# A depthwise convolution split into an input projection and three banded matmuls per output row

## The chip, the core and the metric

The kernel runs on one core of a Trainium2 chip. A core has five engines that matter here, each with its own queue of instructions that it works through strictly in order: PE (TensorE, the matrix engine; its weight loads are listed apart as PEld), DVE (VectorE), ACT (ScalarE), POOL (GpSimd) and SP (SyncE), which issues every DMA of this kernel. Engines wait for each other through semaphores. Data lies in SBUF (128 partitions) and matmuls write to PSUM, which the other engines read.

The metric is the time of one execution on the device in microseconds, as the median of a few executions. Before the change it is 15807.45 us (three executions: 15804.3, 15807.45 and 15817.56).

## The reference, cut to what matters

The input is `x` of shape 2 x 256 x 256 x 128 in fp32. Layer 0 is an attention along each image row; its result is added to `x`. Layer 1, which the change touches, is a selective state-space block:

```python
xz = x @ in_proj_w.T                      # 128 -> 512 channels
xi, z = jnp.split(xz, 2, axis=-1)         # 256 and 256
xi = conv_general_dilated(xi, conv_w, (1, 1), 'SAME', feature_group_count=256) + conv_b
xi = silu(xi)                             # 3x3 depthwise convolution, then silu
...                                       # delta, B, C from xi by small projections
h = dA_t * h + dBx_t                      # 16 states a channel, along all H*W tokens
y = sum over states of h * C + Ds * xi
...                                       # layer norm, times silu(z), projection to 128
```

The input of layer 1 is group-normalised, which the kernel does with one scale and one shift for each of the 128 channels. So for each of 256 inner channels the kernel needs a projection over 128 channels followed by nine taps, three rows by three columns.

## The kernel before, in words

The kernel does layer 0 first, then layer 1 in 128 steps of R = 4 image rows, T = 1024 tokens. Everything is fp32. In the trace one fp32 matmul is two instructions on PE, each with its own weight load.

**Units and slots.** The scan of a step is cut into 32 units of 128 partitions by 1024 tokens: two halves h of 128 channels, in each four groups m of four states, in each four groups q of 32 channels (CQ = 32; 32 channels by SR = 4 states fill the partitions). The last loop of the file (L1130 and following) goes over slots t, one for each unit, and emits the instructions of a slot in a fixed order. Nothing re-orders them later: on PE, DVE, ACT and POOL the program order is the queue order. In a slot come

- the DMAs of six units ahead (`fetch`, on SP);
- `drive`, on POOL, in odd slots: for the pair of units t+3 and t+4 the product `hb` of `du` and `bb` (L1048);
- `products`, on POOL, for five of the 16 pairs of a step, units 6, 14, 22, 26 and 30 with their neighbours (L1084), and a single one for unit 11;
- `decay`, on ACT, for unit t+1: `da` = exp(delta * A) into PSUM (L1038). There are two `da` tiles, so decay of unit t+1 waits until unit t-1 is through with its own;
- `scan` on DVE for unit t (L1060), and, where the unit is not one of POOL's, `product` on DVE (L1075) into `yc`. `yc` tiles hold a pair of units and there are four;
- the pieces of other work that were put into this slot by `at(...)`: first those without `pe=True`, then those with it;
- `start_up` and `add_up` on PE: `add_up` (L1107) sums four units over their states into `y`, and comes in slots 2, 6, 10, 14, ... It frees two of the four `yc` tiles;
- `remember` on ACT, which keeps the last column of the scan (L1065), and at times `y_out`.

**Work put between.** `project(k)` prepares step k: load of the rows, transposes (`turn`), normalisation into `xn` on ACT, then the convolution, the gate `z`, the small projections and three table functions on ACT (`silu_z`, `silu_xs`, `softplus`), each with two table loads. It starts 72 slots before the first scan of its step. `finish_row` does the layer norm and the output of the rows of the step before, from eight slots to eight slots. All pieces of `project` beyond the first step share one PSUM bank ("p"), those of `finish_row` another ("f"): a piece on PE waits until ACT has copied the piece before out of the bank.

In slots counted from 0 to 31 within a step, `project` has its pieces there: `turn` and `normalise` in 24 to 26, the gates in 16 to 18 and 26, `silu_z` in 20, `silu_xs` in 28, the `xd` and `dt` projections in 0 to 3 and 8 to 11, `softplus` in 12. The four convolution blocks of a step (half h by row pair i) begin in slots 27, 3, 11 and 19.

**The convolution before.** The projection and the taps are one set of weights: `w_tap[:, h, tap, :]` is the projection scaled by the tap of each inner channel. A block is nine matmuls (18 instructions) of 128 x 128 weights on 512 columns, shifted windows of `xn`, accumulated in one PSUM tile `u_ps` (L736). They are spread over four slots as 3, 3, 2 and 1 taps; `conv_out` (L747) copies the tile out with the bias five slots after the first. `xn` has two columns of zeros for the border.

## Time and profile before

| what | value |
|---|---|
| executions | 15804.3, 15807.45, 15817.56 us |
| span of the profiled execution, first to last instruction | 15811.9 us, 4.5 us above the median |
| layer 0 and the preparation of the first steps, up to the first scan | 0 to 2631.16 us |
| one step of the scan in the trace, from the scan of unit 11 to that of the next step | 8005.94 to 8108.39 us: 102.45 us |
| convolution matmuls L736, 9216 | 4237.6 us busy, 600 ns each |
| scans L1060, 4096 | 9536.1 us busy, some 2340 ns each |
| decay L1038, 4096 | 4581.5 us busy, 1119 ns each |
| granted TensorE clock | 0.925 on average |

Busy time is the union of the time in which an instruction of the group runs. Matmuls overlap: the end of each is modelled, so the pace of a row of matmuls is read from the starts, and 600 ns is longer than the step from one to the next. In the answers on waits, a line names the waiting instruction, the one that released it, the total in us, the number of times and the longest. In the lines of a timeline the columns are start, duration, engine, source line, operation, what it writes from what, how many; a bracket at the end has the idle time before and what ended it.

### The profile page before, as it was taken

The page shows a single profiled execution, that of the slowest core. Times are in us where ns is not written, and L with a number is a line of the kernel's source. Part 1 is how long each engine was busy: PE and PEld are TensorE (multiplying, and loading weights), DVE is VectorE, ACT ScalarE, POOL GpSimd, SP SyncE. Part 2 cuts the span into 40 slices and gives each one's busy share as a digit, 9 for nine tenths or more (in the row PEclk, how much of TensorE's full clock was granted, in tenths as well). Part 3 has the DMA queues.
Part 4 walks back from the last instruction along what each step waited for, and adds up shares of the span by engine and source line. Part 5 has one row for each costly group of instructions (what it writes and reads, how often), then busy time and mean ns, then how long its engine had stood idle before and what let it go on. Part 6 is the DMA issues. An engine that isn't in the chain of part 4 may idle for free. (4 is left out here: it accounts for less than half of the span.)

```text
span 15811.9 us, 177304 instructions
## 1 busy us (share of the span) xinstructions
PE 13767.7 (87%) x59451; PEld 6979.9 (44%) x59451; DVE 14381.3 (91%) x12134; ACT 10831.9 (69%) x20003; POOL 13322.4 (84%) x3216
## 2 busy tenths in 40 slices
PE   6999998888888888888888888888888888888887
PEld 5877884333333333333333333333333333333333
DVE  6665555999999999999999999999999999999998
ACT  4555555777777777777777677777777777777775
POOL 1111113999999999999999999999999999999998
PEclk8999998999999999999999999999999999999998
DMA  5322223777676776767677667777677777776765
GB/s 194 126 97 82 81 96 121 242 246 240 239 242 241 243 244 241 240 240 245 241 245 244 230 237 244 242 243 244 241 240 243 245 242 243 246 240 241 243 244 194
DMA packets 1426852, 3452.05 MB, mean 218 GB/s; under 512 B 117736, under 2 KB 709136, under 8 KB 1405456
## 3 DMA queue, kind: packets, MB, share of 16 engines
q1 hardware_dynamic: 1425936, 3440.72, 62.7%
q8 instruction: 467, 7.65, 0.2%
q14 instruction: 449, 3.68, 0.1%
HBM read 2752.41 MB, written 687.88 MB: 218 GB/s over the span
## 5 line engine op out<-in xcount | busy, mean ns | idle before, releaser
L1048 POOL TENSOR_TENSOR hb<-du_r,bb 128x2048 f32<-128x2048 f32 x2048 | 9247.5, 4543 | 87.8 <-DMA du_r<-du_d 16.1
L1060 DVE TENSOR_TENSOR_SCAN da<-da,state,hb 128x1024 f32<-128x1024 f32 x2688 | 6301.6, 2344 | 3.5 <-POOL state L1139 3.2
L1038 ACT ACTIVATE da<-delta_r,a_neg 128x1024 f32<-128x1024 f32 x4096 | 4581.5, 1119 | 85.1 <-DMA delta_r<-delta_d 6.0
L736 PE MATMUL u_ps<-xn,w_tap 128*128 128x512 f32 x9216 | 4237.6, 600 | 27.1 <-ACT sz L773 24.1
L1075 DVE TENSOR_TENSOR yc<-da,cc 128x1024 f32<-128x1024 f32 x2688 | 3284.5, 1222 | 253.2 <-PE y L1107 99.1
L1060 DVE TENSOR_TENSOR_SCAN hb<-da,state,hb 128x1024 f32<-128x1024 f32 x1408 | 3234.5, 2335 | 79.6 <-ACT state L1065 65.0
L1084 POOL TENSOR_TENSOR yc<-hb,cc 128x2048 f32<-128x2048 f32 x640 | 2906.8, 4542 | 86.1 <-ACT state L1065 66.4
L736 PEld LDWEIGHTS u_ps<-xn,w_tap 128*128 128x128 f32 x9216 | 1672.3, 190 | 2303.3 <-issue 1862.5
L1107 PE MATMUL y<-yc,sel 128*32 128x512 f32 x16384 | 2408.2, 712 | 20.2 <-POOL yc L1084 19.4
L458 POOL TENSOR_TENSOR x1g<-xc,bo_all 128x512 f32<-128x512 f32 x256 | 316.1, 1275 | 1844.9 <-DVE stats L513 1836.2
L1065 ACT COPY state<-da 128x1 f32<-128x1 f32 x2688 | 426.4, 159 | 1858.9 <-DVE yc L1075 1850.9
L1107 PEld LDWEIGHTS y<-yc,sel 128*32 128x32 f32 x16384 | 492.5, 126 | 1926.2 <-issue 1709.2
L762 PE MATMUL z_ps<-xn,w_z 128*128 128x512 f32 x1024 | 751.6, 825 | 625.5 <-ACT sz L773 316.9
L901 PE MATMUL yt<-centre,ys 128*128 128x256 f32 x4096 | 1030.9, 395 | 265.7 <-ACT ob L971 264.9
L408 ACT ACTIVATE e<-s_ps,nmx 128x256 f32<-128x256 f32 x1024 | 477.1, 476 | 971.8 <-DVE nmx L399 873.6
L804 PE MATMUL dt_ps<-xd,w_dt 8*128 8x512 f32 x1024 | 695.8, 764 | 507.2 <-ACT delta L815 414.1
L1065 ACT COPY state<-hb 128x1 f32<-128x1 f32 x1408 | 268.5, 191 | 1058.0 <-DVE hb L1060 1057.9
L901 PEld LDWEIGHTS yt<-centre,ys 128*128 128x128 f32 x4096 | 742.6, 191 | 445.3 <-ACT ob L971 361.5
L954 PE MATMUL o_ps<-w_out,szr 128*128 128x128 f32 x4080 | 790.0, 275 | 0.0
L954 PE MATMUL o_ps<-w_out,yg 128*128 128x128 f32 x4080 | 789.1, 275 | 0.0
L375 DVE TENSOR_TENSOR v<-v_ps,bv_all 128x512 f32<-128x512 f32 x256 | 176.9, 691 | 581.1 <-PE v_ps L368 581.1
L954 PEld LDWEIGHTS o_ps<-w_out,yg 128*128 128x128 f32 x4080 | 660.4, 192 | 26.9
(162 smaller groups left out, 17185.1 us busy)
## 6 DMA issues: line engine op xcount, KB each, us to landing
bb<-bc_d SPq DMA_DIRECT2D x1024, 512.0 KB, 4.1
cc<-bc_d SPq DMA_DIRECT2D x1024, 512.0 KB, 5.3
delta_r<-delta_d SPq DMA_DIRECT2D x1024, 512.0 KB, 6.3
du_r<-du_d SPq DMA_DIRECT2D x1024, 512.0 KB, 5.2
sz_d<-sz SPq DMA_DIRECT2D x128, 1024.0 KB, 6.5
xs_d<-xs SPq DMA_DIRECT2D x128, 1024.0 KB, 9.5
xr<-xs_d SPq DMA_DIRECT2D x256, 512.0 KB, 6.6
delta_d<-delta SPq DMA_DIRECT2D x128, 1024.0 KB, 8.8
```

The costliest lines, as they stand in the source:

```text
L736: nc.tensor.matmul(o["u"], w_tap[:, h, tap, :], xn[:, i * RB + dy : i * RB + dy + RB, dx : dx + W], start=(tap == 0), stop=(tap == 8),)
L762: nc.tensor.matmul(o["z"], w_z[:, h, :], xn[:, 1 + i * RB : 1 + (i + 1) * RB, 1 : W + 1], start=True, stop=True,)
L804: nc.tensor.matmul(o["dt"], w_dt[:, h, :], o["xd"][0:DR, i * TB : (i + 1) * TB], start=True, stop=True,)
L901: nc.tensor.matmul(o["yt"][:, j, :], ys[k, h][:, t0 + j * P : t0 + (j + 1) * P], centre[:, (1 - h) * P : (1 - h) * P + DI], start=(h == 0) ...
L954: nc.tensor.matmul(o["o"][:, j, :], o[by][:, h, j * P : (j + 1) * P], w_out[:, i, h, :], start=False, stop=(j == WT - 1 and h == NH - 1 an ...
L1038: nc.scalar.activation(da, spreads["delta", k, h, q], AF.Exp, scale=a_neg[:, g, m : m + 1])
L1048: nc.gpsimd.tensor_tensor(hb, spreads["pair", k, h, q], repeats["bb", k, h, m].unsqueeze(1).to_broadcast([P, 2, T]), ALU.mult,)
L1060: nc.vector.tensor_tensor_scan(u["h"], u["da"], u["hb"], st, ALU.mult, ALU.add)
L1065: nc.scalar.copy(st, units[t]["h"][:, T - 1 : T])
L1075: eng.tensor_tensor(u["yc"], u["h"], repeats["cc", k, h, m], ALU.mult)
L1084: nc.gpsimd.tensor_tensor(yc, hb, repeats["cc", k, h, m].unsqueeze(1).to_broadcast([P, 2, T]), ALU.mult)
L1107: nc.tensor.matmul(y[q * CQ : (q + 1) * CQ, cols], sel, units[t + q]["yc"][:, cols], start=False, stop=(m == NSG - 1),)
```

## The change: projection first, then three banded matmuls for each row

The projection and the taps become two sets of matmuls.

- **Weights.** `w_tap` goes. `w_in` is the transposed projection. `w_cv[:, g, r, dx, :]` is a matrix of 128 by 32 for channel group g, output row r of two, and column shift dx: its rows are (input row, channel) for four input rows by 32 channels, and it holds the tap of (dy, dx) where the input row is r + dy and the channels agree. It is built at the start from a zeroed tile `cw`, which six DMAs now fill in place of one, and one multiplication on DVE. 18 scalings on DVE, 18 transposes and 18 copies go, two transposes and copies come.
- **`inner(h, i, j)`**, on PE: for two of the four channel groups, the projection of the four input rows of block (h, i) to 32 channels. Each of eight matmuls has 128 x 32 weights and 256 columns, and writes the 32 partitions of its row: the result has (row, channel) on the partitions.
- **`inner_out(j)`**, on ACT: copies these 128 x 512 values into `xin`, which has the zero border columns that `xn` no longer has.
- **`conv(h, i)`**, on PE: for each of two output rows and three column shifts, four matmuls (one for each channel group, each writing its 32 partitions) of 128 x 32 weights on 256 columns.
- **Slots.** In the first slot of a block: `inner` for j = 0 on PE and, by a new list of pieces that come after those of PE, `inner_out(0)` on ACT. In the second: `inner` for j = 1. In the third: `inner_out(1)`, and then all of `conv`. `conv_out` stays five slots after the first. All of it uses the one bank "p" in turn.
- **Memory.** `xd` moves into the buffer of `raw`, which the load of the next rows uses too.

```diff
+    RB = TB // W
+    w_cv = const.tile([P, NCG, RB, 3, CQ], F32, name="w_cv")
...
+        cw = prep.tile([P, NCG, RB, 3], F32, name="cw")
+        nc.vector.memset(cw, 0.0)
+        taps = conv_w.rearrange("(g c) o i j -> c g (o i) j", c=CQ)
+        for r in range(RB):
+            for dy in range(3):
+                nc.sync.dma_start(
+                    out=cw[(r + dy) * CQ : (r + dy + 1) * CQ, :, r, :], in_=taps[:, :, dy, :]
+                )
...
         for h in range(NH):
-            for tap in range(9):
-                wt = prep2.tile([P, P], F32, name="wt")
-                nc.vector.tensor_scalar(wt, inp[:, h, :], cw[:, h, tap : tap + 1], None, ALU.mult)
-                transposed(w_tap[:, h, tap, :], wt, P)
+            transposed(w_in[:, h, :], inp[:, h, :], P)
...
-        def conv(h, i, taps):
-            if taps[0] == 0:
-                o["u"] = bank([P, RB, W], "u_ps")
-            for tap in taps:
-                dy, dx = divmod(tap, 3)
-                nc.tensor.matmul(
-                    o["u"],
-                    w_tap[:, h, tap, :],
-                    xn[:, i * RB + dy : i * RB + dy + RB, dx : dx + W],
-                    start=(tap == 0),
-                    stop=(tap == 8),
-                )
+        def inner(h, i, j):
+
+            o["xi"] = bank([P, 2, W], "xi_ps")
+            for q in range(2):
+                c = (2 * j + q) * CQ
+                for r in range(SR):
+                    nc.tensor.matmul(
+                        o["xi"][r * CQ : (r + 1) * CQ, q, :],
+                        w_in[:, h, c : c + CQ],
+                        xn[:, i * RB + r, :],
+                        start=True,
+                        stop=True,
+                    )
+
+        def inner_out(j):
+            nc.scalar.copy(xin[:, 2 * j : 2 * j + 2, 1 : 1 + W], o["xi"])
+
+        def conv(h, i):
+            o["u"] = bank([P, RB, W], "u_ps")
+            for r in range(RB):
+                for dx in range(3):
+                    for q in range(NQ):
+                        nc.tensor.matmul(
+                            o["u"][q * CQ : (q + 1) * CQ, r, :],
+                            w_cv[:, h * NQ + q, r, dx, :],
+                            xin[:, q, dx : dx + W],
+                            start=(dx == 0),
+                            stop=(dx == 2),
+                        )
...
-                o["xd"] = s1.tile([64, T], F32, name="xd")
+                xd = s1.tile([P, R, WT, C], F32, name="raw")
+                o["xd"] = xd.rearrange("p r t c -> p (r t c)")[0:64, :]
...
-            for dt, taps in ((0, (0, 1, 2)), (1, (3, 4, 5)), (2, (6, 7)), (3, (8,))):
-                at(t + dt, conv, h, i, taps, pe=True)
+            at(t, inner, h, i, 0, pe=True)
+            at(t, inner_out, 0, after=True)
+            at(t + 1, inner, h, i, 1, pe=True)
+            at(t + 2, inner_out, 1)
+            at(t + 2, conv, h, i, pe=True)
             at(t + 5, conv_out, h, i)
...
-            others, on_pe = slots.pop(t, ((), ()))
-            for piece, args in others:
-                piece(*args)
-            for piece, args in on_pe:
+            others, on_pe, after = slots.pop(t, ((), (), ()))
+            for piece, args in (*others, *on_pe, *after):
                 piece(*args)
```

More of the change, by code (lines that the diff above doesn't have):

```diff
@@ L132, in attn_then_ssm_kernel @@
     lnb_c = columns("lnb_c", ln_b)
-    w_tap = const.tile([P, NH, 9, P], F32, name="w_tap")
+    w_in = const.tile([P, NH, P], F32, name="w_in")
     w_z = const.tile([P, NH, P], F32, name="w_z")
@@ L159, in attn_then_ssm_kernel @@
         nc.sync.dma_start(out=inp, in_=in_proj_w.rearrange("(k p) c -> p k c", p=P))
-        cw = prep.tile([P, NH, 9], F32, name="cw")
-        nc.sync.dma_start(out=cw, in_=conv_w.rearrange("(h p) o i j -> p h (o i j)", p=P))
+        cw = prep.tile([P, NCG, RB, 3], F32, name="cw")
[6 more added lines that the diff above has]
+                )
+        same = prep.tile([P, CQ], F32, name="same")
+        nc.vector.tensor_reduce(
+            same, ident.rearrange("p (r c) -> p c r", c=CQ), AX.X, ALU.add
+        )
+        nc.vector.tensor_tensor(
+            w_cv.rearrange("p g r d c -> p (g r d) c"),
+            same.unsqueeze(1).to_broadcast([P, NCG * RB * 3, CQ]),
+            cw.rearrange("p g r d -> p (g r d)").unsqueeze(2).to_broadcast([P, NCG * RB * 3, CQ]),
+            ALU.mult,
+        )
         outp = prep.tile([P, DI], F32, name="outp")
@@ L631, in attn_then_ssm_kernel @@
     WP = W + 2
-    RB = TB // W
     WT = W // P
@@ L655, in attn_then_ssm_kernel, with at @@
     between = {}
-    def at(t, piece, *args, pe=False):
-        slots.setdefault(t, ([], []))[pe].append((piece, args))
-    xn = s1.tile([P, R + 2, WP], F32, name="xn")
+    def at(t, piece, *args, pe=False, after=False):
+        slots.setdefault(t, ([], [], []))[2 if after else pe].append((piece, args))
+    xn = s1.tile([P, R + 2, W], F32, name="xn")
     nc.gpsimd.memset(xn, 0.0)
+    xin = s1.tile([P, NQ, WP], F32, name="xin")
+    nc.gpsimd.memset(xin, 0.0)
     given = {}
@@ L700, in begin @@
                 if k > 0:
-                    nc.gpsimd.memset(xn[:, 0, 1 : W + 1], 0.0)
+                    nc.gpsimd.memset(xn[:, 0, :], 0.0)
                 first = s1.tile([P, WT, C], F32, name="ob")
@@ L709, in begin @@
             else:
-                nc.scalar.copy(xn[:, 0:2, 1 : W + 1], xn[:, R : R + 2, 1 : W + 1])
+                nc.scalar.copy(xn[:, 0:2, :], xn[:, R : R + 2, :])
             if n < R:
-                nc.gpsimd.memset(xn[:, 2 + n, 1 : W + 1], 0.0)
+                nc.gpsimd.memset(xn[:, 2 + n, :], 0.0)
         def turn(src, r, m):
@@ L723, in normalise @@
             nc.scalar.activation(
-                xn[:, to : to + m, 1 : W + 1],
+                xn[:, to : to + m, :],
                 o["t"][:, 0:m, :],
@@ L729, in normalise @@
             )
-        def conv(h, i, taps):
-            if taps[0] == 0:
-                o["u"] = bank([P, RB, W], "u_ps")
-            for tap in taps:
-                dy, dx = divmod(tap, 3)
-                nc.tensor.matmul(
-                    o["u"],
-                    w_tap[:, h, tap, :],
-                    xn[:, i * RB + dy : i * RB + dy + RB, dx : dx + W],
-                    start=(tap == 0),
-                    stop=(tap == 8),
-                )
+        def inner(h, i, j):
[9 more added lines that the diff above has]
+                        stop=True,
+                    )
+        def inner_out(j):
[11 more added lines that the diff above has]
+                            stop=(dx == 2),
+                        )
         def conv_out(h, i):
@@ L764, in gate @@
                 w_z[:, h, :],
-                xn[:, 1 + i * RB : 1 + (i + 1) * RB, 1 : W + 1],
+                xn[:, 1 + i * RB : 1 + (i + 1) * RB, :],
                 start=True,
```

## The prediction

> **What bounds the kernel now.** I read the page's engine line first, then busy times by stretch, then the waits of DVE and POOL between 4000 and 14000 us (97.6 steps), and last the timelines of one step.

> ```profile
> PE 13767.7 (87%) x59451; PEld 6979.9 (44%) x59451; DVE 14381.3 (91%) x12134; ACT 10831.9 (69%) x20003; POOL 13322.4 (84%) x3216
> 2500.00:15600.00 13100.00, 11298.06 (x45481) 5033.07 (x45482) 12641.47 (x7277) 9334.18 (x16157) 12836.28 (x2913) 0.92 0.70 240
> ...
> DVE yc L1075 <- PE y L1107: 79.3, 99, 1.4
> DVE hb L1060 <- ACT state L1065: 49.8, 96, 0.5
> ...
> POOL yc L1084 <- ACT state L1065: 54.6, 99, 1.8
> ```

> In the scan (second line: PE, PEld, DVE, ACT, POOL, clock, DMA) POOL is busy 98% and DVE 96.5%; PE 86%, ACT 71%. DVE waits 0.8 us a step for PE and 0.5 for ACT, POOL 0.56. So the step of 102.45 us is DVE's row of scans with POOL beside it. PE bounds nothing by its amount: what it does matters only where DVE, or ACT in front of DVE, waits for it.

> Here are slots 10 to 16 of one step; a convolution block begins in slot 11:

> ```profile
> 8004.86 2.07 PE L804 MATMUL dt_ps<-xd,w_dt 8*128 8x512 f32 x2 [2.10 <-ACT delta L815]
> 8006.85 3.33 PE L1107 MATMUL y<-yc,sel 128*32 128x512 f32 x16
> 8010.11 2.84 PE L736 MATMUL u_ps<-xn,w_tap 128*128 128x512 f32 x6
> ...
> 8018.48 1.92 PE L1107 MATMUL y<-yc,sel 128*32 128x512 f32 x16
> ...
> 8008.02 0.68 ACT L815 ACTIVATE delta<-dt_ps,dtb_c 128x512 f32<-128x512 f32 x1
> 8008.59 0.19 ACT L1065 COPY state<-hb 128x1 f32<-128x1 f32 x1
> 8008.67 1.14 ACT L1038 ACTIVATE da<-delta_r,a_neg 128x1024 f32<-128x1024 f32 x1
> 8009.82 1.28 ACT L823 ACT_TABLE_LOAD   x1
> ...
> 8014.53 1.12 ACT L1038 ACTIVATE da<-delta_r,a_neg 128x1024 f32<-128x1024 f32 x1
> ...
> 8011.77 2.35 DVE L1060 TENSOR_TENSOR_SCAN da<-da,state,hb 128x1024 f32<-128x1024 f32 x1
> ...
> 8015.75 4.59 DVE L1060 TENSOR_TENSOR_SCAN hb<-da,state,hb 128x1024 f32<-128x1024 f32 x2
> ```

> See that PE comes to slot 11 only at 8010.11, behind `add_up` of slot 10, while ACT has done slot 11's pieces at 8008.59; and that the `decay` ending at 8015.65 feeds the scan that starts at 8015.75: ACT has no slack there.

> **PE's work.** A block was 18 instructions at some 0.43 us, 8.0 us; four a step, 32 us. It becomes 32 + 48 instructions of 128x32 weights on 256 columns. The nearest row in shape is `y` (128x32, 512 columns):

> ```profile
> 8018.48 0.16 PEld L1107 LDWEIGHTS y<-yc,sel 128*32 128x32 f32 x8 [0.76 <-DVE hb L1060]
> 8018.93 0.13 PEld L1107 LDWEIGHTS y<-yc,sel 128*32 128x32 f32 x4 [0.30 <-issue]
> 8019.36 0.13 PEld L1107 LDWEIGHTS y<-yc,sel 128*32 128x32 f32 x4 [0.30 <-issue]
> ```

> Loads come four together every 0.43 us: four column groups stream side by side, one instruction per 107 ns. With 256 columns I take half, 53 ns. Upper end: 111 ns, the pace of L954 (eight pairs from 8020.87 to 8022.43), since no row shows a load and its matmul going out faster. So `inner` for one j (16) costs 0.85 us (to 1.78), its last result 0.165 us later (592 ns of a `y` matmul less its 427); `conv` (48) costs 2.56 us (to 5.3). A block falls from 8.0 to 4.3 us, some 15 us of PE a step. Alone this is worth nothing: it isn't the bound.
> [...]

> **The added wait.** `inner_out(0)` stands on ACT in the slot in which PE does `inner`. PE reaches that behind `add_up` of the slot before; behind `inner_out(0)` on ACT wait the state copy, the next `decay`, and then often a table function of 4.5 us with the `decay` after it, for which DVE waits. The copy itself costs 0.49 us (the step from the `sz` copy at 8058.94 to the next row at 8059.43).

> - Slot 11: `inner` from 8010.11, result 8011.13; ACT goes on at 8011.65 in place of 8008.59, 3.06 late. `decay`(13) ends 8012.87, so scan 13 goes from 8011.77 to 8012.97. `softplus` follows, `decay`(14) ends 8018.71 instead of 8015.65, scan 14 starts 8018.81: **+3.06 us**.
> - Slot 19: PE's `add_up` of slot 18 lets `inner` start at 8034.31; result 8035.33. ACT's state copy goes from 8034.59 to 8035.85. Scan 21 just holds; `silu_z` follows, and scan 22 (8042.63, already 0.53 late for ACT) becomes **+1.26**.
> - Slot 27: `y` 8058.84 to 8061.71, result of `inner` 8062.73, state copy from 8059.43 to 8063.25. Scan 29 moves from 8062.96 to 8064.56; `silu_xs` follows, scan 30 from 8066.94 to 8070.41: **+3.47**.
> - Slot 3: `y` ends early (8084.94), result 8085.96 against ACT's state copy at 8085.77; no table function follows, `decay`(5) ends by 8088.5 for a scan at 8089.23: **0**.

> Direct sum 7.8 us a step.

> **What is late next.** All of `conv` now waits for `inner_out(1)`, behind that late `decay`: in slot 13 it starts at 8019.25, PE idle since 8012.6. Idle PE restarts slowly here: in the stretch before the first scan, convolution blocks of 18 take 10.12, 9.69 and 9.64 us after gaps, and 7.97 to 8.00 otherwise, so 1.7 to 2.1 us more. I take 4.5 us for `conv` (2.6 to 5.3). Behind it stand `add_up` and the output row.
> - Slot 13: `conv` to 8023.8; the output matmuls end 4.34 later (as 8018.48 to 8022.82 now) at 8028.1, while ACT's `leave`, now 8022.85, would run at 8025.9. ACT wins part of the 2.2 back; at the gate of slot 18 PE is 1.4 behind, which slot 19 hands on in full: **+1.4**.
> - Slot 21: 8043.8 (`decay`(22), with its 1.26) + 0.55 + 4.5 + 1.72 (`start_up`) + 1.9 (`y`) = 8052.5; product 24, which needs that `yc` tile, would run at 8049.57 + 1.26 = 8050.8: **+1.65**. `leave`, the `xn` copy and the normalisations of slots 24 to 26 follow late: scans 26 to 28 lose **0.9**, and product 28's wait for `y` (now 0.76) grows by **0.9**.
> - Slot 29 the same way: no `yc` wait (`y` ends 8077.1, product 0 at 8077.3), but ACT is 1.6 late in slot 0, and slots 3 to 5 lose **1.1**.

> Together 5.9 us a step; nothing if `conv` restarts at full pace.

> **The rest.** POOL and DVE get no work in the scan. ACT's eight copies are in the chains above. SP: the load of `raw` in slot 12 now waits for the `dt` matmul of slot 10, since `xd` lies in the same buffer; behind it are the fetches of six slots ahead, 19 us of cover against 4 to 6 us to land: nothing, and up to 6 us a step without that cover. Before the first scan nine blocks (8 to 10 us) become chains of inner, copy, inner, copy, conv, about 6 to 8: -19 us (-35 to +10). At the start five more DMAs of 0.5 us stand ahead of the loads of x on SP: +3; the scalings and transposes that go lie in DVE's 3.30 us wait for x and give nothing.

> **Sum.** Blocks lie in slots 0 to 4021, 125.7 steps. 125.7 x (7.8 + 5.9) = 1722 us. 15811.9 + 1722 - 19 + 3 = 17518 for the profiled execution, which is 4.5 us (0.03%) above the median of 15807.45: **17515 us**, +10.8%.

> **Rivals.**
> - *Direct stalls alone*: `conv` runs at full pace, its lag is won back in ACT's idle time (ACT waits 2158 us for DVE in the 10000 us). 125.7 x 7.8 - 16 = 964: 16770 us. For it: the clock is granted at 0.92 overall. Against: the gaps of 6 us ahead of `conv`, and slow `y` rows after gaps of 2 us (3.33 for 1.92).
> - *Issue pace*: each load and matmul costs 111 ns. `inner` is 0.9 later in the blocks of slots 11, 19, 27 and 0.4 in slot 3, `conv` 0.8 longer three times: +5.5 us a step, 18200 us. Against: four loads within 0.13 us. That the column groups don't run side by side at all (17 us a block) is excluded by the same rows.
> - *Faster*: PE, 15 us a step lighter, is early everywhere; DVE's 0.8 and ACT's 0.5 go, and POOL, with 54.6 us of waits in 10000, sets the end: 13180 us of scan x 0.55% = 72, about 15735 us. It decides if `inner`'s result is there when ACT comes, that is if PE starts it by 8008.59 - 1.02 = 8007.6 in slot 11. Against: `y` of slot 10 holds PE until 8010.1, behind a `dt` that waits for ACT itself; the change leaves that as it is.
> - *Hidden*: ACT's late `decay` is met by DVE being late too. Against: scan 14 follows its `decay` by 0.1 us.

> **How the numbers follow.** Likeliest case 0.53, its own range 17000 to 17900; direct stalls alone 0.24; issue pace 0.11; smaller stalls, partly absorbed, 0.04; faster 0.06; hidden 0.02. About 0.2% (30 us) is what a measurement here can tell from no change. Slower 0.92, same 0.02, faster 0.06. Range 16550 to 18050: it takes in the direct stalls, and leaves out faster, hidden and the upper half of issue pace.

> **What would show it.** Right: ACT's `xin` copy with idle time released by PE `xi_ps`, 2 to 3 us in slots 11 and 27; DVE's waits for ACT up from 0.5 to 8 us a step or more, at scans 13, 14, 22, 29 and 30; PE's busy share and clock down; POOL under 92% with new waits. `conv` near 4.5 us with slow starts shows the second part, 2.6 the first rival, 5.3 with evenly spaced loads the second. It is wrong if the `xin` copy starts without idle time, or if DVE's waits stay near 1.3 us a step.

## The result, and the profile after

The changed kernel takes **17510.79 us** (median of 17508.42, 17508.69, 17512.89 and 17515.75), against 15806.7 us of the kernel before beside it: a ratio of **1.1077, interval 1.1062 to 1.1092**. The prediction was 17515. One step of the scan, from product 28 to that of the next step, goes from 102.45 to 116.05 us (9000.53 to 9116.58): +13.60, where the prediction's sum was +13.7.

From the page of the changed kernel, the engine line and two of its groups:

```profile
PE 13013.4 (74%) x91179; PEld 6786.8 (39%) x91179; DVE 14474.1 (83%) x12119; ACT 11262.7 (64%) x21011; POOL 13356.8 (76%) x3217
...
L771 PE MATMUL u_ps<-xin,w_cv 128*32 128x256 f32 x24576 | 2383.7, 567 | 2883.3 <-ACT state L1104 2524.1
...
L764 ACT COPY xin<-xi_ps 128x512 f32<-128x512 f32 x1024 | 595.6, 582 | 1227.3 <-PE xi_ps L755 1227.3
```

TensorE is busy for less than before (13013 us, from 13768), DVE and POOL for about the same, and every share has fallen: the engines wait for each other. The granted clock is 0.871 on average, from 0.925. The last column is the idle time ahead of a group. The copies of the inner product wait 1227 us for TensorE, and the convolution stands 2883 us behind waits, nearly all for ScalarE.

The waits of the changed kernel between 4000 and 14000 us (86.2 steps), by DVE, ACT and PE:

```profile
DVE hb L1099 <- ACT da L1077: 519.7, 431, 15.0
DVE yc L1114 <- PE y L1146: 386.2, 345, 2.1
DVE da L1099 <- ACT da L1077: 346.0, 259, 2.0
...
ACT ob L1010 <- PE o_ps L993: 1313.9, 344, 5.6
ACT xin L764 <- PE xi_ps L755: 833.1, 344, 4.1
...
PE u_ps L771 <- ACT state L1104: 1727.2, 258, 7.3
```

Before, DVE waited 0.5 us a step for ACT and 0.8 for PE; now it is (519.7 + 346.0) / 86.2 = 10.0 for ACT's `decay` and 4.5 for `y`. ACT waits 9.7 a step for the inner product, in all four blocks. POOL is busy for 88% of this stretch, from 99%.

Slots 10 to 16 of one step, the place that the prediction showed of before; PE's lines first, then ACT's, then DVE's:

```profile
9052.96 3.64 PE L1146 MATMUL y<-yc,sel 128*32 128x512 f32 x16
9056.38 1.58 PE L755 MATMUL xi_ps<-xn,w_in 128*32 128x256 f32 x16
...
9066.14 5.23 PE L771 MATMUL u_ps<-xin,w_cv 128*32 128x256 f32 x48 [6.40 <-ACT state L1104]
...
9053.54 0.68 ACT L851 ACTIVATE delta<-dt_ps,dtb_c 128x512 f32<-128x512 f32 x1
9058.03 0.58 ACT L764 COPY xin<-xi_ps 128x512 f32<-128x512 f32 x1 [3.81 <-PE xi_ps L755]
9058.51 0.20 ACT L1104 COPY state<-hb 128x1 f32<-128x1 f32 x1
9058.60 1.12 ACT L1077 ACTIVATE da<-delta_r,a_neg 128x1024 f32<-128x1024 f32 x1
9059.74 1.28 ACT L859 ACT_TABLE_LOAD   x1
...
9064.45 1.12 ACT L1077 ACTIVATE da<-delta_r,a_neg 128x1024 f32<-128x1024 f32 x1
...
9056.64 1.22 DVE L1114 TENSOR_TENSOR yc<-da,cc 128x1024 f32<-128x1024 f32 x1 [0.59 <-PE y L1146]
9059.76 2.36 DVE L1099 TENSOR_TENSOR_SCAN da<-da,state,hb 128x1024 f32<-128x1024 f32 x1 [1.90 <-ACT da L1077]
...
9065.67 4.59 DVE L1099 TENSOR_TENSOR_SCAN hb<-da,state,hb 128x1024 f32<-128x1024 f32 x2 [1.85 <-ACT da L1077]
```

Read it from the copy at 9058.03. ACT has been free since 9054.22 and stands for 3.81 us, because `inner` is behind `y`, and both are slow: `y` takes 3.64 us where the row at 9026.82 takes 1.92, `inner` 1.58 where the one at 9028.56 takes 1.05 (the clock granted to TensorE is 0.50 of full speed here, from 9050.63 to 9057.46). Only then come `decay` (to 9059.72; scan 13 starts at 9059.76), the table load and `softplus`, and the next `decay` (to 9065.57; scan 14 starts at 9065.67). And the convolution, which needs the second copy, starts at 9066.14 after 6.40 us without work on PE and takes 5.23 us.

Why so long, the weight loads of another block of the same step show:

```profile
9009.53 0.20 PEld L771 LDWEIGHTS u_ps<-xin,w_cv 128*32 128x32 f32 x8 [6.88 <-ACT state L1104]
9009.96 0.20 PEld L771 LDWEIGHTS u_ps<-xin,w_cv 128*32 128x32 f32 x4 [0.23 <-issue]
9010.39 0.20 PEld L771 LDWEIGHTS u_ps<-xin,w_cv 128*32 128x32 f32 x4 [0.23 <-issue]
...
9012.52 0.20 PEld L771 LDWEIGHTS u_ps<-xin,w_cv 128*32 128x32 f32 x4 [0.23 <-issue]
9012.95 0.62 PEld L771 LDWEIGHTS u_ps<-xin,w_cv 128*32 128x32 f32 x12 [0.23 <-issue]
```

Four loads go out together every 0.43 us for 3.42 us, 107 ns for each load and matmul; from 9012.95 on, 12 take 0.62 us, half of that. The granted clock, asked for in pieces of half a microsecond, says the same: 0.50 from 9006.26 to 9013.08, and 1.00 after. So the pace doubles when the granted clock does; it is not a limit of the issue, since the four of a group come within 0.20 us. In the four blocks of this step the clock rises 3.55, 2.92, 4.97 and 3.90 us after the convolution has begun, and the block at 9066.14, the longest with 5.23 us, is at half pace to its last load. The last section comes back to this.

### The profile page after: what moved, and what is told of

Its sections match the earlier page's. It is cut to its first block, busy times and chain, and to the rows that moved or that the text cites. A ratio compares the mean times of both kernels' runs of the same rounds, so it can differ in the third digit from the quotient of the medians.

```text
span 17506.6 us, 242120 instructions
## 1 busy us (share of the span) xinstructions
PE 13013.4 (74%) x91179; PEld 6786.8 (39%) x91179; DVE 14474.1 (83%) x12119; ACT 11262.7 (64%) x21011; POOL 13356.8 (76%) x3217
## 5 line engine op out<-in xcount | busy, mean ns | idle before, releaser
L771 PE MATMUL u_ps<-xin,w_cv 128*32 128x256 f32 x24576 | 2383.7, 567 | 2883.3 <-ACT state L1104 2524.1
L771 PEld LDWEIGHTS u_ps<-xin,w_cv 128*32 128x32 f32 x24576 | 1039.0, 160 | 4193.8 <-ACT state L1104 2705.7
L1146 PE MATMUL y<-yc,sel 128*32 128x512 f32 x16384 | 2305.9, 684 | 19.5 <-POOL yc L1123 18.7
L1010 ACT COPY ob<-o_ps 128x256 f32<-128x256 f32 x510 | 189.7, 372 | 1909.1 <-PE o_ps L993 1909.1
L764 ACT COPY xin<-xi_ps 128x512 f32<-128x512 f32 x1024 | 595.6, 582 | 1227.3 <-PE xi_ps L755 1227.3
L755 PE MATMUL xi_ps<-xn,w_in 128*32 128x256 f32 x16384 | 1152.0, 402 | 73.1 <-ACT xin L764 5.1
L797 PE MATMUL z_ps<-xn,w_z 128*128 128x512 f32 x1024 | 667.7, 739 | 428.9 <-ACT xn L741 211.0
L840 PE MATMUL dt_ps<-raw,w_dt 8*128 8x512 f32 x1024 | 693.9, 762 | 329.4 <-ACT state L1104 180.0
L755 PEld LDWEIGHTS xi_ps<-xn,w_in 128*32 128x32 f32 x16384 | 507.7, 118 | 817.3 <-issue 325.7
```

Of the source, the lines that this page charges most:

```text
L755: nc.tensor.matmul(o["xi"][r * CQ : (r + 1) * CQ, q, :], w_in[:, h, c : c + CQ], xn[:, i * RB + r, :], start=True, stop=True,)
L771: nc.tensor.matmul(o["u"][q * CQ : (q + 1) * CQ, r, :], w_cv[:, h * NQ + q, r, dx, :], xin[:, q, dx : dx + W], start=(dx == 0), stop=(dx = ...
L797: nc.tensor.matmul(o["z"], w_z[:, h, :], xn[:, 1 + i * RB : 1 + (i + 1) * RB, :], start=True, stop=True,)
L840: nc.tensor.matmul(o["dt"], w_dt[:, h, :], o["xd"][0:DR, i * TB : (i + 1) * TB], start=True, stop=True,)
L1146: nc.tensor.matmul(y[q * CQ : (q + 1) * CQ, cols], sel, units[t + q]["yc"][:, cols], start=False, stop=(m == NSG - 1),)
```

## The experiments

The theory after the result was the prediction's: ACT's wait for the inner product costs about 8 us a step (the direct part), and the convolution, late and at half pace, costs about 5 (the second part). Each is taken away alone, the first is then put into the kernel before, and at the end both are taken away together. All numbers "a step" are the distance to the kernel before in the same comparison, divided by 125.7 steps; the changed kernel stands at 13.6.

**One slot later for the first copy.** Edit against the changed kernel:

```diff
-            at(t, inner_out, 0, after=True)
+            at(t + 1, inner_out, 0)
```

> The changed kernel with one line moved: the first copy of a block, inner_out(0), stands among ACT's pieces of the next slot in place of the end of its own. Nothing else is changed. Theory (the wait of ACT for PE in the slot of the inner product costs 8 to 9 of the 13.6 us that a step grew by, the late conv block most of the rest): ACT no longer waits for xi_ps; what is left is the copy's own 0.5 us ahead of three late decays and part of the late conv block, 3 to 5 us a step, 16200 to 16450 us. Rival (the new matmuls are slow or late in themselves, wherever the copy stands): at least 9 us a step stay, over 16950 us. Rival (the wait alone is the whole loss): under 1 us a step, under 15950 us.

Measured: 16488.23 us, ratio 1.0430 (1.0414 to 1.0445), 38 us above the range. ACT's wait for the inner product falls from 833 to 31 us in the stretch, and 5.4 us a step are left. Moving one copy of each block by one slot wins back 60% of the loss.

**The copy without its wait.**

```diff
         def inner_out(j):
-            nc.scalar.copy(xin[:, 2 * j : 2 * j + 2, 1 : 1 + W], o["xi"])
+            src = o["xi"] if j else xn[:, 0:2, :]
+            nc.scalar.copy(xin[:, 2 * j : 2 * j + 2, 1 : 1 + W], src)
```

> The changed kernel, but the first copy of each block reads xn in place of xi_ps: it stands in the same place and moves as many bytes, and waits for nothing on PE. It leaves out the use of half of the inner product (channel groups 0 and 1 of each half get other values); PE does all of it as before. Theory (the wait): 16400 to 16550 us, the copy's 0.5 us in three blocks and the late conv block stay. Rival (ACT's added work, not its wait): 17300 us or more. ACT's idle time ahead of L764 goes from 833 us in the stretch from 4000 to 14000 us to under 150.

Measured: 16453.54 us (one execution), as expected; 5.1 us a step are left. DVE's waits now:

```profile
DVE yc L1115 <- PE y L1147: 386.7, 271, 3.1
DVE hb L1100 <- ACT da L1078: 189.7, 333, 14.9
DVE da L1100 <- ACT da L1078: 12.5, 36, 1.0
```

The two waits for `decay` go from 866 to 202 us; the wait for `y` stays as it was. The direct part is worth 17510.8 - 16453.5 = 1057 us, 8.4 a step.

**A third of the convolution.**

```diff
-                for dx in range(3):
+                for dx in (1,):
...
-                            start=(dx == 0),
-                            stop=(dx == 2),
+                            start=True,
+                            stop=True,
```

> The changed kernel with a third of the banded matmuls: only the middle column shift, 8 matmuls a block in place of 24, so six of the nine taps are left out. Theory (the conv block of 4.2 to 5.2 us, late behind ACT, costs DVE the waits for yc tiles at units 16 and 24 and some of those at 26 to 28, some 4 us a step; ACT's wait for the inner product stays): a block takes 1.7 us, 16900 to 17150 us. Rival (the length of the block doesn't matter, all of the loss is the direct wait): 17450 us or more.

Measured: 16871.75 us (one execution), 28 below the range. The mirror image of the run before: a block takes 1.07 to 1.94 us, the wait for `y` almost goes (386 to 66 us in the stretch), those for `decay` stay for the most part (866 to 707).

```profile
DVE hb L1099 <- ACT da L1077: 451.9, 410, 12.6
DVE da L1099 <- ACT da L1077: 255.1, 221, 3.1
...
DVE yc L1114 <- PE y L1146: 65.6, 107, 2.2
```

**TensorE kept busy.** The second `inner` is written several times over, the last time with the same numbers, so that PE stands idle for only 1.2 to 1.7 us ahead of the convolution:

```diff
-            for q in range(2):
+            times = (7, 3, 7, 8)[h * NB + i] if j else 1
+            for q in times * (0, 1):
```

> The changed kernel, but the second inner product of a block is done 7, 3, 7 and 8 times over (in the order of the blocks of h and i), with the same result in the same place, so that PE has work until shortly ahead of the conv block. PE does more in all. Theory (a conv block of 48 instructions takes 4.2 to 5.2 us in place of 2.6 because PE stands idle for 3 to 7 us ahead of it): blocks of 2.6 to 3 us, and the time falls by 2 to 4 us a step, to 17000 to 17250 us. Rival (the blocks are slow for another reason, such as the load of 128x32 weights or the reads of xin): blocks as before, 17500 us or more.

Measured: 17002.2 us (16984 to 17041), ratio 1.0752 (1.0734 to 1.077): 21 repeats of the second `inner` in a step, 16 instructions each, make the kernel 509 us faster. One block in PE's timeline:

```profile
9002.79 6.25 PE L756 MATMUL xi_ps<-xn,w_in 128*32 128x256 f32 x112
9010.26 2.80 PE L772 MATMUL u_ps<-xin,w_cv 128*32 128x256 f32 x48 [1.22 <-ACT state L1105]
```

All four blocks of the step take 2.80 us, where they took 4.2 to 5.2 for the same 48 instructions, and the granted clock is 0.948 on average, from 0.871. DVE's wait for `y` falls from 386 to 160. But 9.5 us a step are left, more than the 7.8 of the prediction's direct part alone: DVE still waits 782 us in the stretch for `decay`, 8.8 a step.

**The wait put into the kernel before.** One extra matmul into the bank, a copy of it on ACT in the slot and place where `inner_out(0)` stands, the nine taps as six, two and one from the next slot on; `xd` in the buffer of `raw`, as in the change:

```diff
+        def glance(h, i):
+            o["g"] = bank([P, RB, W], "g_ps")
+            nc.tensor.matmul(
+                o["g"], w_tap[:, h, 0, :], xn[:, i * RB : i * RB + RB, 0:W], start=True, stop=True
+            )
+
+        def seen():
+            nc.scalar.copy(look, o["g"])
...
+            at(t, glance, h, i, pe=True)
+            at(t, seen, after=True)
```

> The kernel before, with the old convolution, and only the wait added: in the first slot of each block PE does one matmul (the first tap, 128x512, 0.86 us and 0.165 us to its result, as the inner product takes) into the bank, and ACT copies its 128x512 values to a tile that nobody reads, in the place of inner_out(0). The nine taps follow in the next slots as six, two and one. xd lies in raw's buffer to make room. Theory (the wait is enough, with the old matmuls too): the 7.8 us a step that were worked out for it before, or up to 10 with what PE does more: 16750 to 17050 us. Rival (the wait is hidden, and the loss came with the new matmuls): under 16000 us.

Measured: 17013.17 us (one execution), 9.6 us a step, in the range. ACT's and DVE's waits:

```profile
ACT look L752 <- PE g_ps L747: 967.7, 357, 4.8
...
DVE hb L1073 <- ACT state L1078: 484.0, 262, 1.9
DVE da L1073 <- ACT da L1051: 370.9, 270, 3.4
DVE yc L1088 <- PE y L1120: 69.9, 157, 2.2
```

The old convolution with a read of PE's result on ACT loses 1206 us, and DVE's wait for `y` stays where it was before (79). So the direct part needs nothing of the new convolution. What was added is a little more than a wait: the copy's own time on ACT and one matmul a block on PE are in the 1206 us.

**The shared buffer alone**, in the kernel before:

```diff
-                o["xd"] = s1.tile([64, T], F32, name="xd")
+                xd = s1.tile([P, R, WT, C], F32, name="raw")
+                o["xd"] = xd.rearrange("p r t c -> p (r t c)")[0:64, :]
```

> The kernel before with one part of the change: xd lies in the buffer of raw. The load of raw then waits on SP for the dt matmul of slot 10. Theory: fetches stand six slots ahead, nothing changes, within 0.2% of before. Rival (SP held up makes delta_r or du_r late): slower by 1 to 6 us a step, 15930 us or more.

Measured: 15806.2 us beside 15806.92, ratio 0.9999 (0.999 to 1.0008). It costs nothing there.

**Two arrangements that should have hidden both parts.** In the first, the pieces move to slots one or two later, and the convolution goes behind `add_up`:

```diff
             at(t, inner, h, i, 0, pe=True)
-            at(t, inner_out, 0, after=True)
-            at(t + 1, inner, h, i, 1, pe=True)
-            at(t + 2, inner_out, 1)
-            at(t + 2, conv, h, i, pe=True)
+            at(t + 2, inner_out, 0)
+            at(t + 2, inner, h, i, 1, pe=True)
+            at(t + 3, inner_out, 1)
+            at(t + 3, conv, h, i, late=True)
```

> The changed kernel with its matmuls and copies as they are, but in other slots: the first copy and the second inner product two slots after the first inner product (so behind the table function and the decay that follows it), the second copy three slots after it, and the conv block there too, but behind add_up, which it now follows on PE. Theory (the loss is only where ACT waits for PE, and what stands behind the late conv block): scans 13, 14, 21, 22, 29 and 30 don't wait more than before, conv starts on a PE that add_up has kept busy and takes about 2.8 us; 0.3 to 2 us a step are left for the output row behind conv, 15850 to 16060 us. Rival (half as much PE work in smaller pieces and eight more copies cost something wherever they stand): over 16400 us. Rival (a lighter PE is worth something once it doesn't stand in the way): under 15770 us, down to the 15735 us that POOL allows.

Measured: 16792.87 us, ratio 1.0623 (1.0605 to 1.064), far off, and slower than moving the one copy. PE's timeline of one block, and one wait of ACT from 4000 to 14000:

```profile
9106.45 1.93 PE L755 MATMUL xi_ps<-xn,w_in 128*32 128x256 f32 x16 [7.77 <-ACT state L1104]
9108.31 2.77 PE L1137 MATMUL y<-xr,d_diag 128*128 128x512 f32 x4
9111.01 1.92 PE L1146 MATMUL y<-yc,sel 128*32 128x512 f32 x16
9112.75 2.77 PE L771 MATMUL u_ps<-xin,w_cv 128*32 128x256 f32 x48
```

```profile
ACT ob L1010 <- PE o_ps L993: 1644.2, 362, 7.5
```

The convolution is at full pace now (2.77 us for its 48), but the slow start has only moved: `inner` waits for the first copy, and after 7.77 us idle it takes 1.93 us (1.05 at 9097.04), and `y` from `xr` behind it 2.77 (1.98 in the changed kernel). The output row stands behind the convolution, and ACT's longest wait for it grows from 5.6 to 7.5 us; scan 26 is 3.05 us late for such a wait in the step from 9000 us.

In the second, the second inner product goes to the other bank ("f"), so that it waits for no copy, both copies come in the fourth slot and the convolution in the fifth:

```diff
-            at(t, inner, h, i, 0, pe=True)
-            at(t, inner_out, 0, after=True)
-            at(t + 1, inner, h, i, 1, pe=True)
-            at(t + 2, inner_out, 1)
-            at(t + 2, conv, h, i, pe=True)
+            at(t + 1, inner, h, i, 0, pe=True)
+            at(t + 2, inner, h, i, 1, pe=True)
+            at(t + 3, inner_out, 0)
+            at(t + 3, inner_out, 1)
+            at(t + 4, conv, h, i, after=True)
```

> The changed kernel with its matmuls and copies as they are, in a third arrangement. The two inner products of a block come in its second and third slot and need no copy between them, since the second takes the bank of the output rows, which is free there; both copies stand in the fourth slot, where ACT has 1 us to spare in the kernel before; conv comes in the fifth, behind add_up and the output row on PE; conv_out stays. Why this is asked: in the arrangement before this one the conv block ran at full pace and scans 13, 14 and 30 no longer waited, yet 7.8 us a step were left; its second inner product waited for a copy, stood in front of start_up and add_up at half pace, and ACT waited up to 6.6 us for the output row behind conv. Theory (that was the same loss in another place: PE waits for ACT, ACT for the output row, DVE for ACT): with nothing of it in front of add_up and the output row, 1 to 3 us a step stay, mostly behind the late conv_out of slot 24, 15930 to 16190 us. Rival (the pieces cost 5 us a step or more wherever they stand): over 16430 us. Rival (all of it hidden, PE's lighter load worth something): under 15770 us.

Measured: 16421.27 us, ratio 1.0388 (1.0371 to 1.0405), 4.9 us a step left. The best of the arrangements with the whole computation, but not the 1 to 3 us expected. The two new waits, of PE and of ACT:

```profile
PE xf_ps L759 <- DVE yg L989: 1539.9, 372, 6.2
...
ACT xs L786 <- PE u_ps L775: 808.0, 371, 2.4
```

`inner` in bank "f" waits for the row that DVE reads out of it, and `conv_out` is the next piece on ACT that stands in front of `decay` waiting for PE.

**Both parts taken away together.** Alone they were worth 1057 us (no wait) and 509 us (full pace) or 639 us (a third). First, the copy without its wait and PE kept busy (the second `inner` 3, 2, 3 and 7 times):

> The changed kernel with the first copy taking its numbers from `xn` instead of the bank (half of the inner product is left unused, so the output is another) and with the second `inner` written 3, 2, 3 and 7 times over, so that TensorE stands idle for little over 1 us ahead of each convolution. Theory (two causes that add: the direct wait, 17510.8 - 16453.5 = 1057 us with that edit alone; the half-pace start of the convolution, 17510.8 - 17002.2 = 509 us with that edit alone): 17510.8 - 1057 - 509 = 15945, from 15850 to 16050. If the late convolution is mostly a consequence of the late decay of the direct wait, removing both gains little more than removing the direct wait: 16250 or more. The convolution is to take 2.8 us where it took 4.4 to 4.8 with the first edit alone.

Then the copy without its wait and a third of the convolution:

> The changed kernel with the first copy taking its numbers from `xn` instead of the bank and with one of the three column shifts in the convolution; half of the inner product and six of nine taps are left out, so the output is another. Theory (the two causes are the whole loss): 17510.8 - 1057 - (17510.8 - 16871.8 = 639) = 15815, from 15730 to 15900; if nothing of PE's is late any more, POOL bounds it and it ends below the kernel before, near the 15735 of the rival 'faster'. If there is a third cost (the load of the next rows behind `xd`, the copies themselves on ACT), it stays above 15950.

Measured: 16280.11 us (ratio 1.0297, 1.0282 to 1.0313) and 16359.87 us (1.0346, 1.0329 to 1.0363). Both are far above the sum: 3.7 and 4.4 us a step are left when ACT does not wait for the inner product and the convolution is at full pace (three blocks of four in the first run) or a third of its length. The theory of two parts that add up to the whole fails. What DVE and ACT wait for in the first of them:

```profile
DVE hb L1101 <- ACT da L1079: 222.5, 333, 13.1
DVE yc L1116 <- PE y L1148: 134.4, 166, 2.2
DVE da L1101 <- ACT da L1079: 63.8, 83, 1.9
...
ACT da L1079 <- DMA delta_r<-delta_d: 277.3, 147, 3.6
```

`decay` is still late, and now waits for its loads (before: 5.2 us in this stretch). That gave two candidates for the rest: the load of `raw`, which waits for `xd`'s readers and stands on SP in front of other loads, and the copies themselves, 0.6 us each on ACT.

**`xd` in its own buffer**, on top of the run with 16280 us:

```diff
-            nc.scalar.copy(xin[:, 2 * j : 2 * j + 2, 1 : 1 + W], src)
+            nc.scalar.copy(xin[:, :, 1 : 1 + W], src)
...
-                            xin[:, q, dx : dx + W],
+                            xin[:, q % 2, dx : dx + W],
...
-                xd = s1.tile([P, R, WT, C], F32, name="raw")
-                o["xd"] = xd.rearrange("p r t c -> p (r t c)")[0:64, :]
+                o["xd"] = s1.tile([64, T], F32, name="xd")
```

> The kernel of the run before (first copy from `xn`, TensorE kept busy; 16280.1 us), with `xd` in a buffer of its own again, so that the load of `raw` does not wait for the `dt` matmuls. To make room, both copies go to the same half of `xin` and all four channel groups read it; the output is another, the instructions and their sizes are the same. That run left 470 us above the kernel before, and ScalarE's `decay` waited 277 us in 10000 for loads of `delta_r`. If the load of `raw`, queued on SyncE in front of those loads, is the third cost: 15850 to 16000. If it is what the copies themselves take on ScalarE (0.6 us each, in front of decays without slack): 16200 to 16300, the same as before.

**No copies**, against the changed kernel:

```diff
         def inner_out(j):
-            nc.scalar.copy(xin[:, 2 * j : 2 * j + 2, 1 : 1 + W], o["xi"])
+            pass
...
-                            xin[:, q, dx : dx + W],
+                            xn[:, q, 0:W],
```

> The changed kernel without the copies at all: the convolution reads `xn` in the same shape and number of matmuls, and nothing reads the inner product, so the output is another. `xd` stays in the buffer of `raw`. TensorE then does all that the change gives it and ScalarE nothing. If the copies' own 0.6 us on ScalarE are the third cost, and all of the loss hangs on ScalarE: 15730 to 15850, bounded by GpSimd. If the load of `raw` behind `xd` is the third cost: 16000 to 16250.

Measured: 16231.3 us (1.027, 1.0255 to 1.0285) and **15823.57 us** (1.0011, 1.0001 to 1.002). The buffer takes away two thirds of the waits for `delta_r` (277 to 96 us) and 49 us of the time: it isn't the third cost. Without the copies all but 17 us of the loss is gone, although PE does all that the change gave it. The two waits of DVE that are longest in total, and one block in PE's timeline:

```profile
DVE yc L1114 <- PE y L1146: 85.9, 101, 1.5
DVE hb L1099 <- ACT state L1104: 58.6, 96, 1.5
```

```profile
9015.31 1.07 PE L755 MATMUL xi_ps<-xn,w_in 128*32 128x256 f32 x16
...
9016.89 1.07 PE L755 MATMUL xi_ps<-xn,w_in 128*32 128x256 f32 x16
9018.05 2.80 PE L771 MATMUL u_ps<-xn,w_cv 128*32 128x256 f32 x48
```

The waits are those of the kernel before (79.3 and 49.8), and the convolution follows `inner` at once and at full pace. So the loss hangs on the way through ACT: that TensorE's product must be read by ACT and given back. This run takes away the wait, the late convolution and the time of the copies at once. How the last 3.4 us a step (16231 against 15807) divide is open. In the run with 16231 us DVE waits some 2.4 us a step for `decay`, 1.7 for `y` (0.8 before) and 0.4 for POOL's `hb`. Two things can make `decay` late there. One is the copies' own time: three of the first copies in a step stand where `decay` had no slack (before scans 14, 22 and 30), and each holds ACT for some 0.5 us, so about 1.5 of it may be theirs, an estimate from the rows (9058.03 to 9058.51). The other is ACT's wait for the output row behind the convolution, 812.9 us in the stretch, where it was 355.0 before; no run takes that away alone. No run with the whole computation came under the kernel before.

## Why the prediction was right, point by point

The time is 4 us from the prediction, and that is partly luck: parts that were too small and parts that were too large cancel. (The sum as worked out gives 17513, not 17515, and takes a copy at 0.52 us in its chains where the text has 0.49; neither matters.) Step by step, in us, from DVE's waits in the step 9000.53 to 9116.58:

| place | predicted | measured |
|---|---|---|
| slot 11: product 12, scans 13 and 14 | 3.06 | 0.59 + 1.90 + 1.85 = 4.34 |
| slots 16 to 22: the 1.4 from slot 18, scan 22 | 1.4 + 1.26 = 2.66 | 0.61 (product 16) + 1.50 - 0.53 = 1.58 |
| product 24 | 1.65 | 2.12 |
| scans 26 to 28 | 0.9 | 0.45 + 0.20 = 0.65 |
| product 28, growth | 0.9 | 1.17 - 0.76 = 0.41 |
| slot 27: scans 29 and 30 | 3.47 | 1.40 + 1.85 = 3.25 |
| slots 3 to 5 | 1.1 | 0.73 |
| sum | 13.7 | 13.1, of 13.6 in all |

- **The direct wait: right, and shown** by the kernel before with this wait and the copy that waits (+1206 us) and by the changed kernel without the wait (-1057 us), 8.4 to 9.6 us a step for the 7.8 predicted. Mis-sized in slot 11: `inner` was put behind the `y` of the old trace and at full pace, but `y` of slot 10 takes 3.64 us where it took 3.33, and `inner` 1.58 where 0.85 was taken: the granted clock was 0.50 until 9057.46. In slot 3 the copy waits too (1.42 us), where the prediction let its result come only 0.2 after the copy's turn; it put the cost there at 0 in this part and at 1.1 in the other, and 0.73 came.
- **The late convolution: the mechanism right**, 4.2 to 5.2 us a block for the 4.5 assumed, at half pace for the first 2.9 to 5.0 us. That the half pace makes the blocks long is shown by the run that keeps PE busy (2.80 us a block, clock 0.948 on average). The rows that the prediction took it from did not show that the gap ahead is the cause: among the blocks before the first scan, those of 7.99 and 8.00 us stand behind gaps of 0.78 and 0.68 us, and the one of 9.69 behind none. One consequence did not come: the lag of 1.4 in slot 18. There the granted clock is 1.00, from 9071.11 to 9091.59, the last `z` takes 1.13 us and `y` 1.92 where they took 1.65 and 3.04 before, and scan 21 waits for nothing. In its place product 16 waits 0.61.
- **"Nothing if `conv` restarts at full pace": wrong.** With all four blocks at 2.80 us the kernel is at 17002, not at the 16770 that the rival "direct stalls alone" gave. The direct part is larger than its 7.8 (DVE waits 8.8 us a step for `decay` there), and the convolution is late even at full pace, since it waits for a copy behind a late `decay`: DVE waits 1.8 us a step for `y`, 0.8 before.
- **The split of the sum, 7.8 and 5.9 as two terms that add: wrong, and the total does not show it.** Taken away together the parts give 1151 to 1231 us and not 1566 to 1696. This fits one chain of PE and ACT that runs through the step, in which the next link holds DVE where one is shortened (ACT's waits for loads came up when both parts were gone); the chain as such is argued, not shown. The copies' own time was inside the direct term (0.49 each) and stays when the wait goes.
- **Issue pace: excluded**, as the four loads within 0.20 us and the full pace of 2.80 us for 48 pairs (under 59 ns each) show.
- **Faster: not reached even without the copies.** PE was busy 10% less (7752 us in the stretch for 8651) and the time was 0.1% above before: PE's amount is worth nothing here, as the prediction had it.
- **The rest.** The shared buffer at nothing was right for the kernel before, and a buffer of its own won 49 us in the one other kernel in which it was tried (there both copies also went to one half of `xin`). The work ahead of the first scan was mis-sized: -19 + 3 predicted, but the first scan starts at 2637.98 instead of 2631.16, so it is +7: the chains of inner, copy, inner, copy, conv were put at 6 to 8 us and take up to 11.8 (2588.40 to 2600.21), where the second copy stands behind a table function on ACT.

## What to carry to other kernels

When work is split so that another engine must read a result and hand it back, price the round trip first: where that engine's queue is in order and stands in front of the bottleneck, the read costs what is queued ahead of it on the producer (8.4 to 9.6 us a step here), and the work that follows starts late (the convolution after up to 7.3 us without work on PE). Less work on an engine that is not the bound bought nothing here (PE 10% less busy without the copies, time 0.1% up), and the way to it cost much, most of all through one copy a block in the wrong slot. Shares found by taking one part away at a time need not add when the parts lie on one chain: run them away together before calling the account closed.

## What was not expected of the hardware

The prediction tied the slow start to the gap ahead of it. The fall to half pace does not go by the length of the gap alone: in the run without the wait and with PE kept busy, a block at 9006.28 after 3.17 us idle takes 2.80 us, and one at 9059.02 after 2.06 us idle takes 4.48, and changes pace in the middle of its work:

```profile
9059.02 0.65 PEld L773 LDWEIGHTS u_ps<-xin,w_cv 128*32 128x32 f32 x16 [2.54 <-ACT state L1106]
9059.89 0.22 PEld L773 LDWEIGHTS u_ps<-xin,w_cv 128*32 128x32 f32 x4 [0.21 <-issue]
9060.31 0.22 PEld L773 LDWEIGHTS u_ps<-xin,w_cv 128*32 128x32 f32 x4 [0.21 <-issue]
```

Sixteen loads come at full pace, then four every 0.43 us. The granted clock, asked for in pieces of half a microsecond, shows when the pace changes. In the two steps read it is 0.50 or 1.00, but for the pieces in which it changes, and these give the time of the change (0.76 from 9006.00 to 9006.50, after 1.00 and before 0.50: 9006.26):

| kernel | changes of the clock, us (falls in bold) |
|---|---|
| changed | **9006.26**, 9013.08, **9033.56**, 9036.98, **9050.63**, 9057.46, **9064.29**, 9071.11, **9091.59**, 9098.42, **9112.07**, 9115.48 |
| without the wait, PE kept busy | **9045.84**, 9052.67, **9059.49**, 9062.90, **9100.45**, 9107.28 |
